# First image of phase 1: a hand-written order, a norm on VectorE and ScalarE, and v's bias outside the matmuls

## The chip, the core and the metric

The kernel runs on one core of one Trainium2 chip. The metric is the device time of one execution in microseconds (us), and the comparison is made on the median of several runs. The engines are called by the profile's names: PE is TensorE (PEld its weight loads), DVE is VectorE, ACT is ScalarE, POOL is GpSimd, SP is SyncE, which here only issues DMAs. Each engine executes its own queue in order.

## What is computed

Two attention layers follow each other on x of shape (8, 512, 32, 32). The change touches only the first step of the first layer: group norm, the q, k and v projections, and the extremes of q, k and v, which the quantisation afterwards needs. Cut to that:

```python
h = group_norm(x.reshape(b, c, T), gn_w, gn_b)          # 32 groups of 16 channels, T = 1024
qkv = jnp.einsum('oc,bct->bot', qkv_w, h) + qkv_b[None, :, None]
q, k, v = jnp.split(qkv.reshape(b * NUM_HEADS, -1, T), 3, axis=1)
q, k, v = fake_quant(q), fake_quant(k), fake_quant(v)   # 8 bits, scale from the whole tensor's min and max
w = softmax(einsum('bct,bcs->bts', q * scale, k * scale))
```

The scale of each quantisation comes from all of q, k or v, so q, k and v of all eight images are computed and stored to DRAM first (phase 1), and attention starts only then.

## The kernel before

**Tiles.** The channels of an image are 4 chunks of 128 partitions (`CC = 4`), its 1024 tokens two halves (`hf`, 512 each). The loop over images and halves is at the end of phase 1 (from line 675); within a half it calls `blocks` (line 663). A block is one output tile of 128x512. For q and k a block is a group of 128 output channels, for v it is 128 tokens. A matmul of the projection is done with split operands: `split_weights` (line 424) and `split_half` (line 435) make of weights and normed x a high part (ACT), a low part and a mix (DVE, two rows each), and for the weights ACT scales the low part. `three` (line 487) then does 8 matmuls into a bank `a` and 4 into a bank `m`; `put` (line 499) has ACT make u from bank a, with the scale -(SH+1) and a bias, and DVE combine u with bank m and take the running maximum. `store` (line 507) takes the minimum on DVE and issues the store on SP. PSUM is one pool of eight banks (`one`, line 393).

**Image 0.** Two of the four q groups and two of the four k groups are done with unsplit matmuls in fp32 (`qk_mm`, line 587: four fp32 matmuls over the chunks per tile, each of which the trace shows as two), since these don't need the split weights. The rest of image 0 is done as blocks (`blocks`, line 663, where b is 0): in each half two q, two k and four v blocks. The later images have twelve blocks in each half. The first two tiles of q (`early`) run chunk by chunk, while the norm of the next chunk is still under way: `norm_steps` (line 225) takes the statistics of a chunk (`bn_stats`, twice, and an aggregate, on DVE), averages over the groups with a matmul against `gavg` (gps), forms the deviation with four small DVE rows, averages again (gps2), adds eps (DVE), takes the power -0.5 on POOL (line 260), multiplies by the weight and applies mean and scale to x on DVE, two halves of 512.

**Biases.** `bias(i)` (line 564) folds the norm's bias into q's, k's and v's: four matmuls of 32 columns (wt), a copy by ACT, and a sum over channels (wc, q and k) or rows (wr, v). For v the result is written in fp32r as `vrow`: high part in partitions 0 to 31, the remainder in 32 to 63. `pick` is a matrix with two rows of ones. `v_block` (line 527) passes `(pick, vrow)` to `three` as a ninth matmul of bank a:

```python
pairs.insert(0, first)          # line 492: the bias as a matmul of its own, in v blocks alone
```

**Order.** PE's order is the program's: `mm` chains each matmul to the last (line 206). The other engines' orders are made when the kernel is built, by a scheduler that takes rows whose inputs it holds for ready. `InOrder` (line 72) wraps DVE, ACT and PE; only if `InOrder.planned` is set does it chain each instruction to the one before. In phase 1 before the change it isn't set. What order there is comes from generators: `several` (line 611) yields the steps of the split of half 0, six weight parts and half 1, and `go` takes steps of it between blocks; `norm(b + 1)` (as `ahead`) is taken a step per block, so that the two averages of image 1 stand in PE's queue between blocks of image 0. `dve.after(normed)` keeps the splits of image 0 behind its norm. SP takes its DMAs in order. At the start these are x and weights of q by chunks (lines 420, 422), the weights of k and v (line 545), then x of image 1; v's bias is loaded from ACT's queue. Two buffers of the pool `raw` hold the bias stage first, and later the first q and k of phase 2, which SP loads ahead.

## Time and profile before

| | us |
|---|---|
| median of 3 runs (lowest, highest) | 2612.9 (2612.3, 2613.9) |
| the profiled execution, its own time | 2613.4 |
| its span in the trace | 2611.6 |
| phase 1, from the start to the last v block of image 7 | about 591 |
| PE busy of the span | 2546.6 (98%) |
| DVE, ACT, POOL busy | 1863.7 (71%), 1389.8 (53%), 195.3 (7%) |

In the trace all instructions of DVE and ACT carry line 91 (the recording wrapper) and all matmuls line 206, so instructions are told apart by the tiles they write and read: `qkps<-x,raw_w` is an unsplit matmul of image 0, `qkps<-half,w_high` a split one, `vps<-vrow,pick` the bias of v, `gps_a` an average over groups, `gst_a` a statistics row, `gmv_a` an aggregate, `u_ring` and `u_last` the tile u. A matmul's length in the trace overlaps that of the next, so distances are taken from start to start. The granted clock of PE is given as a share of full speed. "Idle before" is the time in which the engine had nothing before this row, and the name behind it what ended that.

### The profile page before, as it was taken

To read this page: it belongs to the slowest core of one execution; us is meant where nothing else is said; L and a number is where in the kernel's file an instruction comes from. 1 tells how busy PE (TensorE), PEld (TensorE's weight loads), DVE (VectorE), ACT (ScalarE), POOL (GpSimd) and SP (SyncE) were. 2 spreads that over 40 slices of the span, in tenths; PEclk is the share of its full clock that TensorE was granted. 3 is DMA by queue.
4 is the path that set the end of the run, shared out by engine and by line. 5 is a ranking of instruction groups with operands and counts; after the bars stand their busy time and mean duration, and the time that the engine had idled before them with its cause. 6 is when DMAs were issued, how large, how long until landed. Compare 5 with 4: busy or idle time off the path is not lost.

```text
span 2611.6 us, 38765 instructions
## 1 busy us (share of the span) xinstructions
PE 2546.6 (98%) x15670; PEld 1763.3 (68%) x15670; DVE 1863.7 (71%) x2675; ACT 1389.8 (53%) x1750; POOL 195.3 (7%) x160
## 2 busy tenths in 40 slices
PE   7899999998989999999999999999999999999998
PEld 4788888882236775776677577757766775777687
DVE  7766666558777777877777777778777776776544
ACT  3333333326866674666576566746665765664121
POOL 0000000001110001000100010010001000100000
PEclk9999999999999999999999999999999999999999
DMA  5333233333421222223312322322232123212211
GB/s 177 142 123 112 112 117 129 122 125 102 137 67 44 64 98 92 76 86 102 102 46 78 122 82 66 106 82 86 74 109 98 54 78 118 86 46 89 86 37 38
DMA packets 154958, 242.05 MB, mean 93 GB/s; under 512 B 26512, under 2 KB 92048, under 8 KB 153232
## 3 DMA queue, kind: packets, MB, share of 16 engines
q1 hardware_dynamic: 124064, 181.50, 21.2%
q10 hardware_dynamic: 30704, 57.97, 6.5%
q8 instruction: 125, 2.05, 0.3%
q14 instruction: 65, 0.53, 0.1%
HBM read 152.59 MB, written 86.28 MB: 91 GB/s over the span
## 4 chain that ended last, share of the span: by engine, by line
PE 88%; DVE 4%; ACT 3%; issue 2%; DMA 1%; POOL 0%; SPq 0%; ACTq 0%; DVEq 0%; POOLq 0%
PE s L206 15%; PE o L206 13%; PE qkps L206 13%; PE pj L206 9%; PE av L206 8%; PE v2ps L206 7%; PE vps L206 7%; PE g L206 7%; PE st L206 4%; PE sm L206 4%; ACT pt L91 1%; PE fold L206 1%; DVE two L91 1%; DVE acc L91 1%; ACT aside L91 1%
## 5 line engine op out<-in xcount | busy, mean ns | idle before, releaser
L91 ACT ACTIVATE pt<-st,esc 128x1024 f32<-128x1024 f32 x496 | 526.8, 1114 | 344.1 <-PE st L206 325.0
L91 DVE TENSOR_TENSOR two<-pt,two 128x1024 f16<-128x1024 f32 x496 | 596.9, 1220 | 134.1 <-POOL two L906 110.0
L91 ACT CAST two<-pt 128x1024 f16<-128x1024 f32 x358 | 362.3, 1056 | 5.1 <-ACT p L91 5.1
L906 POOL CAST two<-pt 128x1024 f16<-128x1024 f32 x128 | 169.8, 1327 | 1545.4 <-ACT pt L91 780.6
L206 PE MATMUL av<-two,v 128*32 128x512 f16 x3968 | 244.7, 381 | 0.0
L206 PE MATMUL s<-g,h 128*128 128x256 f32 x1024 | 233.4, 380 | 0.0
L206 PE MATMUL pj<-ao,wp 128*128 128x512 f32 x512 | 223.8, 595 | 0.0
L206 PEld LDWEIGHTS s<-g,h 128*128 128x128 f32 x1024 | 192.9, 190 | 31.0 <-issue 4.3
L206 PE MATMUL st<-q,k 64*128 64x512 bf16 x1024 | 164.0, 383 | 25.0 <-ACT pt L91 12.9
L206 PEld LDWEIGHTS <-v 128*32 128x32 f16 x3968 | 91.2, 96 | 136.3 <-issue 63.4
L206 PE MATMUL s<-g,sums 128*128 128x256 f32 x768 | 178.5, 381 | 0.2 <-DVE p L91 0.2
L206 PEld LDWEIGHTS pj<-ao,wp 128*128 128x128 f32 x512 | 96.0, 190 | 121.5 <-issue 111.3
L206 PE MATMUL o<-p,v 128*128 128x256 f32 x768 | 175.2, 382 | 0.9 <-DVE p L91 0.9
L206 PEld LDWEIGHTS o<-p,v 128*128 128x128 f32 x768 | 144.3, 190 | 27.1 <-issue 5.7
L206 PEld LDWEIGHTS s<-g,sums 128*128 128x128 f32 x768 | 144.5, 190 | 24.4 <-issue 4.6
L206 PE MATMUL sm<-two,ones 128*32 128x512 f16 x1984 | 136.2, 379 | 0.6 <-ACT rs L91 0.6
L91 ACT ACTIVATE u_ring<-qkps,qkbt 128x512 f32<-128x512 f32 x89 | 60.9, 684 | 140.4 <-PE qkps L206 130.7
L206 PEld LDWEIGHTS <-k 64*128 64x128 bf16 x1024 | 34.7, 94 | 147.8 <-issue 144.6
L206 PE MATMUL qkps<-half,w_high 128*128 128x512 f32 x480 | 130.5, 394 | 0.0
L206 PE MATMUL qkps<-half,w_mix 128*128 128x512 f32 x480 | 129.5, 392 | 0.0
L206 PE MATMUL qkps<-half,w_low 128*128 128x512 f32 x480 | 129.4, 391 | 0.0
L206 PE MATMUL g<-h,wa 128*128 128x256 f32 x512 | 122.7, 388 | 2.0 <-DVE h L91 1.9
(209 smaller groups left out, 3871.3 us busy)
## 6 DMA issues: line engine op xcount, KB each, us to landing
rs<-rs_d SPq DMA_DIRECT2D x80, 256.0 KB
x<-in_x_dram SPq DMA_DIRECT2D x32, 512.0 KB
q_d<-wa SPq DMA_DIRECT2D x32, 512.0 KB
k_d<-wa SPq DMA_DIRECT2D x32, 512.0 KB
raw<-q_d SPq DMA_DIRECT2D x32, 512.0 KB
raw<-k_d SPq DMA_DIRECT2D x32, 512.0 KB
v_d<-v_ring SPq DMA_DIRECT2D x32, 512.0 KB
x_d<-h SPq DMA_DIRECT2D x64, 256.0 KB
```

The costliest lines, as they stand in the source:

```text
L91: ins = self.latest = op(*args, **kw).ins
L206: ins = nc.tensor.matmul(ps, lhsT=lhsT, rhs=rhs, **kw).ins
L906: copy(two[:, 0], pt)
```

## The change

1. `InOrder.planned` is set from before the first load to the end of image 0's first half, so DVE and ACT keep the written order among the rows of that stretch; rows of what comes afterwards are still placed by the scheduler. The order itself is written out: per chunk `stats0`, `centre0`, `spread0`, then splits, weight parts, extractions and stores.
2. In image 0's norm the power on POOL is replaced: ACT takes the square root, DVE the reciprocal and one correcting step (`spread0`); mean and scale are applied by ACT, but for chunk 0's first half. The later images keep POOL's power.
3. The first halves of q's and k's weights (512 KB each) are not split in image 0. `load_rest` loads them again, into the two buffers of the pool `raw`, and `split_rest` splits them as a side job of image 1's first half. So that image 1 doesn't need them at once, images from 1 on take the group pairs in the order 1, 0.
4. v's bias: no matmul with `pick`; `vrow` holds -SH times the bias in fp32 in all partitions, and `put` has DVE make u for v, with `vrow` as a full operand. For q and k u stays with ACT.
5. The load of v's bias goes from ACT's queue to SP's, behind the weights; three memsets on POOL and two copies on ACT are gone.

The weight sums `wt`, `wc` of k and `wt`, `wr` of v are called in other places of PE's order. The diff, cut to what the text speaks of:

```diff
-            def three(nm, left, right, first=None):
+            def three(nm, left, right):
 
                 a, m = (one(f"{nm}_{i}") for i in range(2))
                 pairs = [(left[i][cc], right[i][cc]) for i in range(2) for cc in range(CC)]
-                if first is not None:
-                    pairs.insert(0, first)
                 for i, (lt, rt) in enumerate(pairs):
                     mm(a, lhsT=lt, rhs=rt, start=(i == 0), stop=(i == len(pairs) - 1))
                 for cc in range(CC):
...
             def put(dst, a, m, bias, name):
                 i = turn_of("u", 3)
                 u = u_ring[:, i, :] if i < 2 else u_last
-                act.activation(u, a, AF.Identity, bias=bias, scale=-(SH + 1.0))
+                if name == "vmax":
+                    dve.scalar_tensor_tensor(u, a, -(SH + 1.0), bias, ALU.mult, ALU.add)
+                else:
+                    act.activation(u, a, AF.Identity, bias=bias, scale=-(SH + 1.0))
...
-                        (pick, vrow),
                     )
-                    put(t[:, i, :], a, x, 0.0, "vmax")
+                    put(t[:, i, :], a, x, vrow, "vmax")
                     yield
...
+            InOrder.planned = True
             load_x(0)
...
-            act.dma_start(vb, vbias[0:1, :].partition_broadcast(P))
+            nc.sync.dma_start(vb, vbias[0:1, :].partition_broadcast(P))
...
                 if i == 2:
                     dve.tensor_add(vb, vb, by_row())
-                    dve.tensor_scalar(vb, vb, SH / (SH + 1.0), None, ALU.mult)
-                    act.copy(vrow, vb)
-                    dve.tensor_tensor(
-                        vrow[32:64, :], vb[32:64, :], vrow[32:64, :].bitcast(F32), ALU.subtract
-                    )
+                    dve.tensor_scalar(vrow, vb, -SH, None, ALU.mult)
                     return
...
+            def centre0(c):
+                d, mean, *_ = cols0(c)
+                ps = one(f"gps_a0_{c}")[:, 0:1]
+                mm(ps, lhsT=gavg, rhs=mv0[:, c, 0:1], start=True, stop=True)
+                dve.tensor_sub(d, mv0[:, c, 0:1], ps)
+                dve.tensor_copy(mean, ps)
+                dve.tensor_mul(d, d, d)
+                dve.tensor_add(d, d, mv0[:, c, 1:2])
+
+            def spread0(c):
+                d, mean, var, root, rstd, step, off = cols0(c)
+                ps = one(f"gps2_a0_{c}")[:, 0:1]
+                mm(ps, lhsT=gavg, rhs=d, start=True, stop=True)
+                act.activation(root, ps, AF.Sqrt, bias=eps)
+                dve.tensor_scalar(var, ps, EPS, None, ALU.add)
+                dve.reciprocal(rstd, root)
+                dve.scalar_tensor_tensor(step, var, rstd, rstd, ALU.mult, ALU.mult)
+                dve.tensor_scalar(step, step, -0.5, 1.5, ALU.mult, ALU.add)
+                dve.scalar_tensor_tensor(
+                    rstd, rstd, vec[:, V_GN0W + c : V_GN0W + c + 1], step, ALU.mult, ALU.mult
+                )
+                dve.scalar_tensor_tensor(off, mean, -1.0, rstd, ALU.mult, ALU.mult)
+                for hf in range(NH):
+                    xx = x0[:, c, bass.ts(hf, 512)]
+                    if (c, hf) == (0, 0):
+                        dve.tensor_scalar(xx, xx, rstd, off, ALU.mult, ALU.add)
+                    else:
+                        act.activation(xx, xx, AF.Identity, bias=off, scale=rstd)
...
-            part = norm(0, CC)
-            early = [[one(f"qkps_0_{t}_{hf}") for hf in range(NH)] for t in range(2)]
-            for g in (*part, part[0], part[0], part[1]):
-                next(g)
-            bq, bk, bv = (bias(i) for i in range(3))
-            then = iter((part[1], part[2], part[2], part[3], part[3]))
-            for cc in range(CC):
-                for t in range(2):
-                    for hf in range(NH):
-                        qk_mm(early[t], t, hf, cc)
-                        if (cc, hf) in ((0, 1), (1, 0), (1, 1)):
-                            next(next(then, iter(())), None)
-                            normed = dve.latest
-                if cc >= 2:
-                    next(bq, None)
...
+            first = split_half(0, 0)
+            stats0(0, 0)
+            stats0(0, 1)
+            centre0(0)
+            stats0(1, 0)
+            spread0(0)
+            stats0(1, 1)
+            centre0(1)
+            stats0(2, 0)
+            early_mm(0, 0)
+            spread0(1)
+            early_mm(0, 1)
+            stats0(2, 1)
+            centre0(2)
+            stats0(3, 0)
+            first[0]()
+            early_mm(1, 0)
+            spread0(2)
+            early_mm(1, 1)
+            stats0(3, 1)
+            centre0(3)
+            first[1]()
+            early_mm(2, 0)
+            spread0(3)
+            next(bq)
+            early_mm(2, 1)
+            first[3]()
+            first[2]()
+            parts[0][0]()
+            parts[1][0]()
+            first[4]()
+            early_mm(3, 0)
+            early_mm(3, 1)
+            first[5]()
+            next(bq, None)
+            parts[0][1]()
+            parts[2][0]()
+            parts[3][0]()
+            parts[1][1]()
+            outs = [[out_tile() for _ in range(NH)]]
+            late = [one(f"qkps_0_{PAIRS}_{hf}") for hf in range(NH)]
+            for hf in range(NH):
+                for cc in range(CC):
+                    qk_mm(late, PAIRS, hf, cc)
+            for t in range(2):
+                for hf in range(NH):
+                    out_of(early[t], outs[0], t, hf)
+            next(bk)
+            parts[0][2]()
+            parts[1][2]()
+            parts[2][1]()
+            next(bk, None)
+            keep(outs[0], 0, 0)
+            outs.append([out_tile() for _ in range(NH)])
+            last = [one(f"qkps_0_{PAIRS + 1}_{hf}") for hf in range(NH)]
+            for hf in range(NH):
+                for cc in range(CC):
+                    qk_mm(last, PAIRS + 1, hf, cc)
+            for hf in range(NH):
+                out_of(late, outs[1], PAIRS, hf)
+            next(bv)
+            parts[2][2]()
+            parts[3][1]()
+            parts[3][2]()
+            next(bv, None)
+            second = split_half(0, 1)
+            for step in second[:3]:
+                step()
+            keep(outs[0], 0, 1)
+            for hf in range(NH):
+                out_of(last, outs[1], PAIRS + 1, hf)
+
+            def chores():
+                keep(outs[1], 1, 0)
+                yield
+                yield from one_by_one(second[3:])
+                keep(outs[1], 1, 1)
+                yield
+
...
+            rest = []
+
+            def load_rest():
+                for i in range(2):
+                    t = raw_p.tile([P, T], F32, tag="raw", name=f"rest_{i}").rearrange(
+                        "p (c n) -> p c n", c=CC
+                    )
+                    cs = slice(i * C, i * C + C // 2)
+                    nc.sync.dma_start(t, w_qkv[:, :, cs])
+                    rest.append(split_weights(t, slice(0, CC), cs))
+
+            def split_rest():
+                for i in range(2):
+                    rest[i][0]()
                     yield
-                yield from split_half(0, 1)
-
-            more = several()
+                    rest[i][1]()
+                    yield
+                    rest[i][2]()
...
-            go(more, 6)
-            for isk in range(2):
-                outs = [out_tile() for _ in range(NH)]
-                for t in range(2):
-                    if isk:
-                        ps = [one(f"qkps_0_{PAIRS + t}_{hf}") for hf in range(NH)]
-                        for hf in range(NH):
-                            for cc in range(CC):
-                                qk_mm(ps, PAIRS + t, hf, cc)
-                    else:
-                        ps = early[t]
-                    if (isk, t) == (0, 1):
-                        go(bk)
-                    elif (isk, t) == (1, 0):
-                        go(bk)
-                        go(bv)
-                    elif (isk, t) == (1, 1):
-                        go(bv)
-                    c = isk * PAIRS + t
-                    for hf in range(NH):
-                        dve.tensor_scalar(
-                            outs[hf][:, t, :], ps[hf], qkb[:, c : c + 1], None,
-                            ALU.add, ALU.max, accum_out=column("kmax" if isk else "qmax"),
-                        )
...
             def blocks(b, hf):
                 if b == 0:
@@ -667,7 +777,7 @@
                     for n in range(2):
                         yield from v_block(b, hf, n)
                     return
-                for m in range(2):
+                for m in (1, 0):
...
-                            side = [more, more, ahead]
+                            ahead = behind(3, ahead)
+                            side = [chores(), ahead]
                         else:
-                            side = [split_half(b, 1), ahead]
+                            side = [one_by_one(split_half(b, 1)), ahead]
+                            if b == 1:
+                                side.insert(0, split_rest())
...
+                        if b == 0:
+                            load_rest()
...
+                InOrder.planned = False
```

## The prediction

> **What bounds the kernel now.** I read the share of each engine by stretches first. Columns: stretch, its length, then busy time and instruction count of PE, PEld, DVE, ACT and POOL, the granted PE clock, the DMA share, GB/s.
>
> ```profile
> 15.00:53.00 38.00, 36.82 (x115) 16.56 (x116) 31.12 (x63) 13.47 (x15) 1.65 (x3) 1.00 0.35 132
> 53.00:67.60 14.60, 14.60 (x63) 11.45 (x61) 14.44 (x24) 7.76 (x10) 0.00 (x0) 1.00 0.44 144
> 67.60:74.50 6.90, 0.06 (x1) 0.01 (x1) 6.90 (x13) 0.00 (x0) 0.00 (x0) 0.72 0.55 166
> 110.00:590.00 480.00, 479.94 (x2095) 390.99 (x2094) 305.85 (x585) 161.01 (x217) 6.05 (x6) 1.00 0.33 123
> ```
>
> From 110 to 590 us (images 1 to 7 of phase 1) PE never rests, and DVE is busy 64%: here time is what PE has to do. In image 0 it is otherwise: DVE is full from 53 to 74.5, and PE stands for 6.9 us. The list of waits and the timeline say for whom (columns: start, length, engine, what, idle before it and its releaser):
>
> ```profile
> PE gps_a L206 <- DVE gmv_a L91: 16.0, 3, 7.0
> ```
>
> ```profile
> 13.46 0.54 POOL L260 TENSOR_TENSOR grstd_a<-grstd_a,mhalf 128x1 f32<-128x1 f32 x1
> ...
> 14.83 3.78 PE L206 MATMUL qkps<-x,raw_w 128*128 128x512 f32 x4 [3.29 <-DVE x L91]
> ...
> 53.07 1.49 PE L206 MATMUL qkps<-half,w_high 128*128 128x512 f32 x4
> ...
> 53.67 0.69 DVE L91 TENSOR_TENSOR stage<-stage,wr 128x512 f32<-128x512 f32 x1
> ...
> 74.18 0.20 DVE L91 BATCH_NORM_AGGREGATE gmv_a<-gst_a 128x2 f32<-128x12 f32 x1
> ...
> 74.52 0.56 PE L206 MATMUL gps_a<-gmv_a,gavg 128*128 128x4 f32 x2 [6.86 <-DVE gmv_a L91]
> ...
> 75.51 1.91 PE L206 MATMUL vps<-w_high,half 128*128 128x512 f32 x4
> ```
>
> PE executes in order. The group average of image 1 (gps_a) stands in its queue in the middle of image 0, and its input is the last of a long DVE list. After the stop the four matmuls take 1.91 us, later 1.09.
>
> The steady part, one v block to the next:
>
> ```profile
> 207.64 0.39 PE L206 MATMUL vps<-vrow,pick 128*128 128x512 f32 x1
> 207.87 1.10 PE L206 MATMUL vps<-w_high,half 128*128 128x512 f32 x4
> ...
> 209.74 1.09 PE L206 MATMUL vps<-w_mix,half 128*128 128x512 f32 x4
> ...
> 210.67 0.40 PE L206 MATMUL vps<-vrow,pick 128*128 128x512 f32 x1
> ```
>
> A v block takes 3.03 us, and the bias matmul 0.23 of it (207.64 to 207.87; lengths overlap, so starts are compared).
>
> **What the Trainium skill says.** "TensorE: Matmul & The Clock Gate", section "What's actually happening": after an idle window of about 3.4 us the array runs at half clock until it has been busy as long again. The trace agrees: half speed from 14.83 to 18.6, and from 75.1 to 80.8. "VectorE: DVE Perf Modes", "Why PSUM operands drop a tier": an fp32 operand in PSUM holds DVE at one element a cycle. The trace agrees: PSUM plus SBUF at 128x512 is 0.69 us (53.67 above), a plain SBUF multiplication of that size 0.42. "ScalarE: Activation LUTs", "What ACT_TABLE_LOAD costs" and "Table sets: the hidden batching unit": 1.28 us and a drain of 1.38 for each change of set, and exp and sqrt are in different sets. The trace has one load of 1.28 us; no run shows the drain.
>
> **The change, part by part.** Times are those of the profiled execution, 2613.4 us (span 2611.6), 0.5 above the median 2612.9; differences carry over to the median. Orders are those of the built program.
>
> *v's bias.* 64 matmuls go, 8 in image 0. In images 1 to 7: 56 x 0.23 = 12.9 us off a PE that never rests. In return u of the v blocks moves from ACT (0.60 us) to DVE. The trace has no such instruction; the nearest row is 0.69 us (start to start 0.61, the next row begins at 54.28). Bounds 0.6 and 0.8; I take 0.65. That is 56 x 0.65 = 36 us, and DVE goes from 306 of 480 to some 340 of 467, 73%. Its cover is the eight PSUM banks, four blocks of two: PE may run on while a u is late. Cost taken: 0. Without this cover each us of lateness would be one of PE.
>
> *Norm of chunk 0 without GpSimd.* Before, the power waits for GpSimd, whose first result starts at 12.73, and PE begins at 14.83. After: the second average is there at 8.8 as before, ACT takes the root (0.3, between 0.2 and 0.5). DVE first has a statistics row of chunk 1, whose data came at 9.37; v's bias no longer loads ahead of it (256 KB), so about 8.9. Then 0.65 + six small rows 0.9 + half of x 0.55 = 11.05. But PE's queue has the first average of chunk 1 ahead, which needs one more statistics row and the aggregate (0.8): 11.9, and 0.6 for it. **PE begins at 12.5**, 2.3 us sooner.
>
> *The rounds after it.* A round is: average (0.3), four small rows (0.65), meanwhile two half-tile matmuls, second average (0.25), root (0.3), six small rows (0.9), statistics and aggregate (0.8). The root stands behind the two matmuls in PE's order, so DVE idles here; in return ACT, not DVE, applies seven of eight halves (DVE saves 7 x 0.54). Aggregates come at 11.9, 18.6 (half clock) and 22.9, chunk 2's second pair ends at 27.8, chunk 3's four at 31.2. Before: 34.9. Gain 3.7.
>
> *Weight sums for k and v* now stand directly ahead of what reads them: wt, copy on ACT (0.6 with its wait), wc. PE waits 0.65 us twice. Before, 7 us of matmuls lay between. PE from 31.2: wc 0.85, eight matmuls 6.9, wt 0.95, 0.65, wc 0.85, 6.9, wt 0.95, 0.65, wr 0.86 = 19.6. So **the split blocks begin at 50.8**, before 53.07.
>
> *What DVE has left then.* The row that adds wr to v's bias now stands ahead of all of hf 1's split, so DVE waits for wr about 3 us, until 50.8. From there to the last aggregate of image 1, by DVE's order, start-to-start times of the trace: 12 rows of 1024 (two split pairs, w_low and w_mix of the moved q weights, which the scheduler pulls in here, six minima) x 1.135 = 13.6; two extractions 1.3; seven maxima 4.4; three u 1.95; statistics 14 x 0.60 = 8.4 (six of image 2, pulled in too); six aggregates 0.7; bias rows 0.9; a wait for ACT's `half`, behind two w_low scalings, 1.2. Sum **32.5 us: 83.3**. Before: 53.67 to 74.3, 20.6 us.
>
> *What that makes late.* gps_a now stands after all eight blocks. PE has them done at 50.8 + 4 x 2.75 + 4 x 2.8 = 73, and then stands about **10 us**, to 83.3. The average takes 0.6, hf 1 begins at 83.9, at half clock for 5.7 us as before: 2.85 lost, so it counts as 86.75. Before, hf 1 began at 87.01 at full clock. **The first half of image 0 gains 0.25 us**: the start's gain goes into the longer stop. Then image 1's norm is late: applied by ACT from 92.1 (before 83.8), its last split row at 113.0, by the same addition; image 1's first block starts at 109.0 and wants it at 111.7, and a low part 0.35 sooner. **Loss 1.65 us**, taken whole.
>
> *Queues.* SP gets two 512 KB weight loads ahead of k's first stores; the load that prefetches phase 2's first q waits for their split, and image 2's x stands behind that. DVE reads image 2 six rows after its buffer is free, 6 us; in the trace such a load was read 4.6 us after issue without a wait. Cost 0; if it were 3 us late, 3 us. The root on ACT is followed by nothing urgent. The power of the later images stays on GpSimd.
>
> *End of phase 1.* A second table load stands ahead of the first exp. ACT is idle from 600.1 to 601.5 there, so 1.28 us fits; with the skill's drain, 1.3 late. On the other side the last v maximum has one row of 0.69 less ahead of it: 0.5. Taken: 0, bounds -0.5 and 1.3.
>
> Sum: 12.9 + 0.25 - 1.65 = 11.5; 2613.4 - 11.5 = 2601.9, against the median **2601.4**.
>
> **Rivals.** *A: the start keeps its gain.* Were DVE's list no longer than before beyond PE's blocks (a stop of 7 us, no wait in image 1), it would be 12.9 + 8 x 0.23 + 2.3 = 17: 2596. For it: my rows may be long by 5%, 1.6 us. Against it: the counted rows. *B: image 0 loses more.* Loads of image 2 or the moved weights land late, or chunk 1 lands at 9.4: 3 to 6 us, 2606. For it: DVE waits in order, and all of its list is critical. *C: slower than before.* DVE's u in the v blocks: bank a comes free only when DVE gets to it. It decides from the point where DVE is more than two blocks (5.6 us) behind PE; were each of the 56 delayed by 0.5 us, 28 us: 2629. Against it: DVE in the steady part shows idle times of 1 to 2 us in most blocks, so it catches up. *D: no change*, if image 0 loses all the 11.5: 2613. That the matmuls are gone is plain from the program.
>
> **Numbers.** Forecast 60%, own range 2597.5 to 2604; A 19%, B 13%, C 4%, D 4%. Likeliest 2601.4. The range goes down to A's 2595 and up past B to 2607.5. Measurement tells about 0.2%, 5 us: faster by more is below 2607.7, that is forecast, A and most of B: 0.90; within 0.06; slower 0.04.
>
> **What would show it.** A v block of 2.80 us, PE full from 115 to the end of phase 1; PE's first x matmul near 12.5 and split blocks near 50.8; one stop of PE of about 10 us ahead of gps_a, half clock after it; a pause near 110; a table load at the end of the phase with pt right behind. Wrong it would be by a v block of over 2.9 us with PE waiting for DVE's u, or by a stop that is not there.

## The result, and the profile after

| | before | changed |
|---|---|---|
| median of 8 runs each | 2613.4 us (2610.7 to 2616.2) | 2605.9 us (2604.1 to 2606.6) |
| ratio, 95% interval | | 0.9969 (0.9958 to 0.998) |
| span of the profiled execution | 2611.6 us | 2604.0 us |

The change makes the kernel 0.3% faster: 7.5 us by the medians, 7.6 between the two profiled executions. The prediction was 2601.4 us, 11.5 us less than before, in a range of 2595 to 2607.5; its forecast proper, without the rivals, reached from 2597.5 to 2604.

First the share of each engine by stretches of the changed kernel (stretch, length, busy time and count of PE, PEld, DVE, ACT and POOL, granted PE clock, DMA share, GB/s):

```profile
15.00:51.00 36.00, 33.48 (x112) 14.76 (x112) 26.15 (x60) 14.94 (x21) 0.00 (x0) 1.00 0.30 116
51.00:73.00 22.00, 22.00 (x95) 17.52 (x94) 20.57 (x33) 9.05 (x11) 0.00 (x0) 1.00 0.80 264
73.00:83.50 10.50, 1.01 (x5) 0.48 (x3) 10.50 (x25) 0.00 (x0) 0.00 (x0) 0.68 0.18 71
110.00:580.00 470.00, 467.98 (x2027) 379.31 (x2028) 339.42 (x637) 126.28 (x161) 6.04 (x6) 1.00 0.34 125
```

DVE has gone from 64% to 72% of the steady part and PE is still full there, as predicted. The stop of PE in image 0 is now 73 to 83.5, while DVE works through. PE's list of waits in the first 600 us (what waits, for what, sum, times, longest), and its timeline in image 0:

```profile
PE gps_a L206 <- DVE gmv_a L91: 20.3, 5, 9.5
...
PE qkps L206 <- DVE half L91: 1.6, 2, 1.1
...
PE gps_a L206 <- DVE gd_a L91: 1.0, 2, 0.5
PE wr L206 <- ACT stage L91: 0.8, 1, 0.8
PE wc L206 <- ACT stage L91: 0.7, 1, 0.7
```

```profile
12.01 2.91 PE L206 MATMUL qkps<-x,raw_w 128*128 128x512 f32 x3
...
51.24 1.50 PE L206 MATMUL qkps<-half,w_high 128*128 128x512 f32 x4
...
83.54 0.59 PE L206 MATMUL gps_a<-gmv_a,gavg 128*128 128x4 f32 x2 [9.53 <-DVE gmv_a L91]
83.98 2.05 PE L206 MATMUL qkps<-half,w_high 128*128 128x512 f32 x4
85.84 1.64 PE L206 MATMUL qkps<-half,w_low 128*128 128x512 f32 x4
...
107.91 1.10 PE L206 MATMUL qkps<-half,w_high 128*128 128x512 f32 x4
...
110.00 0.74 PE L206 MATMUL qkps<-half,w_low 128*128 128x512 f32 x2 [0.53 <-DVE half L91]
...
112.27 0.74 PE L206 MATMUL qkps<-half,w_mix 128*128 128x512 f32 x2 [1.05 <-DVE half L91]
112.84 0.85 PE L206 MATMUL qkps<-half,w_high 128*128 128x512 f32 x3
```

The start is there at 12.01 and the split blocks at 51.24; the gain is gone at 83.54, after a stop of 9.53 us; four matmuls take 1.86 us from there to 85.84, about half speed; 110.00 and 112.27 are image 1 waiting for its split rows. At 112.84 image 1's second block begins. In the kernel before, the first block of image 1 began at 110.12 and took 2.75, so its second began at 112.87. **At this point the two kernels are level.** The line of before, and then DVE's side in the changed kernel:

```profile
110.12 1.09 PE L206 MATMUL qkps<-half,w_high 128*128 128x512 f32 x4
```


```profile
51.84 0.69 DVE L91 TENSOR_TENSOR stage<-stage,wr 128x512 f32<-128x512 f32 x1 [4.09 <-PE wr L206]
...
83.30 0.19 DVE L91 BATCH_NORM_AGGREGATE gmv_a<-gst_a 128x2 f32<-128x12 f32 x1
```

**Where the 7.6 us come from.** The marks below are starts in the profiled executions. "Folding" is the first matmul after the last v block of phase 1.

| | image 0's second half | image 1's first block | its first v group | folding | folding to the end |
|---|---|---|---|---|---|
| before | 87.01 | 110.12 | 121.12 | 592.37 | 2019.2 |
| changed | 83.98 | 107.91 | 121.09 | 583.14 | 2020.8 |

Image 0 gives nothing, images 1 to 7 give 9.2 us, and 1.6 us are lost after phase 1. From image 1 on PE takes turns: a q/k group of four blocks (48 matmuls), then a v group of two blocks (24 matmuls). The 9.2 need a closer look, because the v groups do shrink as predicted: from 6.05 to 5.60 us each, and 28 of them make 12.6 us. What takes back 3.4? The timeline of PE in the changed kernel, a q/k group at 144.51 and the next at 161.31:

```profile
141.71 1.09 PE L206 MATMUL vps<-w_high,half 128*128 128x512 f32 x4
142.65 1.09 PE L206 MATMUL vps<-w_low,half 128*128 128x512 f32 x4
143.58 1.10 PE L206 MATMUL vps<-w_mix,half 128*128 128x512 f32 x4
144.51 1.10 PE L206 MATMUL qkps<-half,w_high 128*128 128x512 f32 x4
145.45 1.10 PE L206 MATMUL qkps<-half,w_low 128*128 128x512 f32 x4
146.38 1.10 PE L206 MATMUL qkps<-half,w_mix 128*128 128x512 f32 x4
...
161.31 1.09 PE L206 MATMUL qkps<-half,w_high 128*128 128x512 f32 x4
162.24 1.08 PE L206 MATMUL qkps<-half,w_low 128*128 128x512 f32 x4
163.16 1.07 PE L206 MATMUL qkps<-half,w_mix 128*128 128x512 f32 x4
```

Read the starts, not the lengths. From 145.45 to 146.38 four matmuls take 0.93 us, 233 ns each; from 162.24 to 163.16 they take 0.92, and over the whole group 229. The same group in the kernel before (it starts at 145.02), 0.92 us for four:

```profile
145.95 1.08 PE L206 MATMUL qkps<-half,w_low 128*128 128x512 f32 x4
146.87 1.07 PE L206 MATMUL qkps<-half,w_mix 128*128 128x512 f32 x4
```

There all q/k groups of 48 matmuls take 11.00 us, or 11.09 behind an average of the next image's norm; in the changed kernel 13 of them take 11.20 (144.51 is the first, 548.25 the last), with the granted clock at 1.00 and no wait in the list. That is 2.6 us. Two v groups with a part of the next image's norm in them also stop for DVE's `gd_a` (1.0 us for the two in the list of waits), so that 0.45 + 0.70 us of the 12.6 do not arrive. Ahead of the first stop, at 127.6 us, DVE has waited 1.35 us for a load of x; ahead of the second, at 464.5, a row of u stands before the last row of `gd_a`. 12.6 - 2.6 - 1.15 = 8.85; the rest to 9.2 is rounding and the step to the folding.

### The profile page after: what moved, and what is told of

Same layout as the page of the kernel before. It is cut to its first block, busy times and chain, and to the rows that moved or that the text cites. A ratio compares the mean times of both kernels' runs of the same rounds, so it can differ in the third digit from the quotient of the medians.

```text
span 2604.0 us, 38580 instructions
## 1 busy us (share of the span) xinstructions
PE 2532.2 (97%) x15606; PEld 1750.0 (67%) x15606; DVE 1905.0 (73%) x2748; ACT 1358.1 (52%) x1696; POOL 194.1 (7%) x153
## 4 chain that ended last, share of the span: by engine, by line
PE 85%; DVE 4%; ACT 3%; issue 2%; DMA 2%; POOL 0%; SPq 0%; ACTq 0%; DVEq 0%
PE s L206 15%; PE o L206 14%; PE qkps L206 11%; PE pj L206 9%; PE av L206 8%; PE v2ps L206 7%; PE g L206 7%; PE vps L206 5%; PE st L206 4%; PE sm L206 4%; ACT pt L91 1%; PE fold L206 1%; DVE two L91 1%; ACT aside L91 0%; DVE acc L91 0%
```

## The experiments

All ratios are to the kernel before, run on the same chip as the variant: its median was 2612.6 us beside experiments 1 to 4, 2613.1 beside 5 to 8 and 2612.5 beside 9 to 12. The theory I started from: PE's matmuls have two paces, and the pace is handed on from group to group; the bias matmul used to break the chain. The rivals: the pace belongs to the new order of the column halves (`for m in (1, 0)`), or to the place in the half image.

**1. v's bias by VectorE, alone** (on the kernel before).

```
-                act.activation(u, a, AF.Identity, bias=bias, scale=-(SH + 1.0))
+                if name == "vmax":
+                    dve.scalar_tensor_tensor(u, a, -(SH + 1.0), bias, ALU.mult, ALU.add)
+                else:
+                    act.activation(u, a, AF.Identity, bias=bias, scale=-(SH + 1.0))
...
-                        (pick, vrow),
-                    put(t[:, i, :], a, x, 0.0, "vmax")
+                    put(t[:, i, :], a, x, vrow, "vmax")
...
+                    dve.tensor_scalar(vrow, vb, -SH, None, ALU.mult)
```

> The kernel before, with v's bias added by VectorE and nothing else of the change. Theory (the pace of the q and k matmuls is handed over from block to block: a v group of 24 equal matmuls leaves every second q/k group at 233 ns a matmul, and the bias matmul, which stood ahead of each v block, used to bring it back to 229): 12.6 us come off images 1 to 7, about 2.6 of them are lost again to q/k groups at 233 ns, and image 0 loses some 1.5 because its list on VectorE gets 2 us longer: about 2605, with half of the q/k groups of images 2 to 7 at 11.20 us instead of 11.00. Rival (the slower pace belongs to the new order of the two halves of the q and k columns, and not to the bias): all q/k groups stay at 11.00 us, and the time is about 2602.5.

Measured: 2601.7 us, ratio 0.9965 (0.9952 to 0.9979). 13 q/k groups take 11.20 us, with the column halves in their old order: the rival falls. But image 0 did not lose 1.5 us, it gained 2.7: image 1's first v group starts here:

```profile
118.42 1.10 PE L206 MATMUL vps<-w_high,half 128*128 128x512 f32 x4
```

Before, it was 121.12. 1.9 us of that come from image 0's first v group and 0.9 from its second. My fear that u on DVE would lengthen the stop was wrong: it is 6.3 us here, before 6.9.

**2. The order of image 0 without the bias** (on the changed kernel; the bias matmul, its `pick` and its `vrow` as before).

```
+                        (pick, vrow),
-                    put(t[:, i, :], a, x, vrow, "vmax")
+                    put(t[:, i, :], a, x, 0.0, "vmax")
...
+            act.copy(pick, picked)
```

> The changed kernel with v's bias back as a matmul on TensorE: only the new order of image 0, the split of weights in image 1, and the swapped order of column halves are left. Theory: all q/k groups are at 11.00 us again, v groups at 6.05; image 0 gains about 1 us, because its list on VectorE is 2 us shorter than in the changed kernel; about 2612, no difference that counts. Rival (the pace belongs to the order of the column halves): every second q/k group stays at 11.20 us and the time is about 2615.

Measured: 2620.0 us, ratio 1.0028 (1.0017 to 1.004). All q/k groups but those of image 0 and image 1's first are at 11.00 to 11.09, as the theory has it, but this run does not isolate the order: my edit put a wait at the head of it. ACT and DVE at the start:

```profile
14.66 0.43 POOL L568 MEMSET stage<- 1x128 f32 x2
15.12 0.30 ACT L91 CAST pick<-stage 128x128 fp32r<-128x128 f32 x1 [12.67 <-POOL stage L568]
15.44 1.28 ACT L91 ACT_TABLE_LOAD   x1
16.73 0.26 ACT L91 ACTIVATE root<-gps_a,eps 128x1 f32<-128x1 f32 x1
17.03 0.16 DVE L91 TENSOR_SCALAR var<-gps_a 128x1 f32<-128x1 f32 x1 [8.39 <-ACT root L91]
```

In a written order ACT cannot take the root before the copy ahead of it, the copy waits for GpSimd, and DVE loses 8.4 us. The split blocks began at 59.48 instead of 51.24.

**3. The column halves in the old order** (on the changed kernel).

```
-                for m in (1, 0):
+                for m in (1, 0) if (b, hf) == (1, 0) else (0, 1):
```

> The changed kernel, with the column halves of the q and k weights in the order of before (first, second) from the second half of image 1 on. Theory (handed-over pace): the slow q/k groups stay where they were, the first group of each half image, whichever columns it reads; time as the changed kernel, 2605.9. Rival (the second half of the columns, by its place in memory, is read more slowly): the slow groups move to the second place of each half image.

Measured: 2605.0 us, ratio 0.9973 (0.9962 to 0.9985). Neither text is right in full. In image 1 the slow group was the second of the half image, from 211.99 on it was the first, and after a v group with a stop for `gd_a` (458.33, 6.67 us instead of 5.97) there was no slow group any more up to the end of the phase, though nothing interrupted PE any further. So the pace is bound neither to the columns nor to the place: a pattern that is there goes on, which is what "handed on" means. Behind an interruption it can change but need not: in the changed kernel the v group at 458.10 has the same stop and the same 6.67 us, and every second group stays slow after it.

**4. VectorE's later rows held back** (on the changed kernel; `first_norm[0]` is the row that writes image 1's `goff`).

```
                     dve.bn_stats(st[:, i, hf, :], src(cc, hf))
+                    if nm == "a2":
+                        dve.after(first_norm[0])
...
                     dve.tensor_tensor(low, raw, high.bitcast(F32), ALU.subtract)
+                    if wait:
+                        dve.after(first_norm[0])
```

> The changed kernel; VectorE's statistics rows of image 2 and its rows that split the remaining q and k weights are held back until image 1's norm has its factors. Theory (TensorE's stop in image 0 is set by VectorE's list alone): some 6 us of rows leave that list, image 1's last aggregate comes at about 77.2 instead of 83.3, the second half of image 0 starts at about 78, image 1's first block 3 to 6 us sooner; about 2601. Rival (the rows that were held back meet the splits of image 1 in turn, so that image 1 starts no sooner): the stop is shorter, but image 1's second block still starts at about 112.8, and the time is 2605.9.

Measured: 2606.7 us, ratio 0.9981 (0.9972 to 0.9989). The rival is right. Image 0's second half starts at 79.59 (changed: 83.98), image 1's first block at 104.28 (107.91), and then PE stands for image 1's second pair of split rows:

```profile
104.28 1.10 PE L206 MATMUL qkps<-half,w_high 128*128 128x512 f32 x4
105.22 0.62 PE L206 MATMUL qkps<-half,w_low 128*128 128x512 f32 x2
110.13 1.22 PE L206 MATMUL qkps<-half,w_low 128*128 128x512 f32 x2 [4.29 <-DVE half L91]
```

Its first v group starts at 122.42, 1.3 us later than in the changed kernel. The rows that left one stretch met the next one.

**5. DVE does not wait for wr** (on the changed kernel).

```
             next(bv)
-            parts[2][2]()
             parts[3][1]()
+            second = split_half(0, 1)
+            second[0]()
+            parts[2][2]()
             parts[3][2]()
-            next(bv, None)
-            second = split_half(0, 1)
-            for step in second[:3]:
-                step()
             keep(outs[0], 0, 1)
             for hf in range(NH):
                 out_of(last, outs[1], PAIRS + 1, hf)
+            second[1]()
+            second[2]()
+            next(bv, None)
```

> The changed kernel, in which VectorE takes the rows that wait for wr (v's bias) behind the minimum, the maxima and the first split pair of image 0's second half, and ScalarE writes that half's first part ahead of two scalings of w_low. Theory (what image 0 loses is VectorE's idle time ahead of wr, 4.1 us, plus 0.5 for the split's input): its list to image 1's last aggregate ends some 3.4 us sooner, at about 80; image 1's second block starts at about 109.4 instead of 112.84; about 2602.5. Rival (as in the run with rows held back: what sets image 1's start is the whole of VectorE's rows up to there, and idle time of VectorE later on grows by the same amount): image 1's second block stays at 112.8 and the time at 2606.

Measured: 2607.6 us, ratio 0.9975 (0.9967 to 0.9984); image 1's first v group starts at 124.80. The wait for wr is gone, and DVE's list is no shorter: one row waits 1.83 us for a load of x, one 0.56 us for PE, one 1.39 us for ACT's `half` (0.52 in the changed kernel), and ahead of image 1's last aggregate stand an aggregate of image 2 and a row of the remaining weights, 1.2 us. DVE at its end:

```profile
82.73 0.19 DVE L91 BATCH_NORM_AGGREGATE gmv_a<-gst_a 128x2 f32<-128x12 f32 x1
82.84 1.17 DVE L91 TENSOR_TENSOR w_low<-rest,w_high 128x1024 fp32r<-128x1024 f32 x1
83.93 0.20 DVE L91 BATCH_NORM_AGGREGATE gmv_a<-gst_a 128x2 f32<-128x12 f32 x1
```

Part of what is freed goes to other waits, part to a row that the scheduler puts in. My theory gave no place to either, and fell.

**6. A small matmul in the v group** (on the changed kernel).

```
                 a, m = (one(f"{nm}_{i}") for i in range(2))
+                if kick:
+                    mm(a[:, 0:4], lhsT=gavg, rhs=vec[:, 0:4], start=True, stop=True)
...
+                        kick=b > 0 and (n, i) == (0, 1),
```

> The changed kernel with one more matmul of four columns (a group average of constants, written to a bank that the block then overwrites; it leaves nothing out) ahead of the last v block of each half image from image 1 on. Theory (handed-over pace: a matmul of another shape inside the v group ends the lock, as the bias matmul did): all q/k groups of images 1 to 7 at 11.00 us, 13 x 0.2 = 2.6 us gained against 14 x 0.09 = 1.3 us for the added matmuls: about 2604.5, and the trace decides. Rival (the pace depends on the mean length of a v group, or on something else than a matmul of another shape): the slow groups at 11.20 us stay, and the time is about 2607.

Measured: 2606.3 us, ratio 0.9972 (0.9962 to 0.9983). **From image 1's second q/k group on each of them takes 11.00 us** (11.09 in those behind a norm's average). PE's timeline across the added matmul into the group that was slow:

```profile
141.86 0.28 PE L206 MATMUL vps<-vec,gavg 128*128 128x4 f32 x2
142.00 1.18 PE L206 MATMUL vps<-w_high,half 128*128 128x512 f32 x4
...
144.88 1.09 PE L206 MATMUL qkps<-half,w_high 128*128 128x512 f32 x4
145.80 1.08 PE L206 MATMUL qkps<-half,w_low 128*128 128x512 f32 x4
146.72 1.08 PE L206 MATMUL qkps<-half,w_mix 128*128 128x512 f32 x4
```

Its price was mis-estimated: the v group grows from 5.60 to 5.82, by 0.22 us and not 0.09, so that 14 of them take 3.1 us for 2.6.

**7. The same on the first experiment**: v's bias by VectorE in the old order, with `kick=b > 0 and (n, i) == (1, 1)`.

> The kernel before with v's bias added by VectorE (the first experiment) and the matmul of four columns ahead of the last v block of each half image from image 1 on. Theory: the q/k groups are all at 11.00 us, some 1.3 us net faster than the first experiment: about 2600.5. Rival: slow groups stay; about 2603.

Measured: 2603.9 us, ratio 0.9962 (0.9949 to 0.9976). One slow group is left, image 1's first, ahead of the first added matmul. The folding begins at 579.89, against 579.68 without the matmul: here too its price (3.1 us by the figure above) is more than its gain of 2.6.

**8. The order of image 0 alone, mended**: as 2, with the copy moved.

```
-            act.copy(pick, picked)
...
+                    act.copy(pick, picked)
                     act.copy(vrow, vb)
```

> As the second experiment (the changed kernel with v's bias as a matmul again), but with ScalarE's copy of the selecting matrix moved from the start to just ahead of v's bias, so that ScalarE's root no longer stands behind it. Theory: PE's first matmul on x is at about 12 us again, all q/k groups at 11.00 us; the order of image 0 alone is worth about nothing: image 1's second block starts at 111 to 113, and the time is about 2612. Rival (the written order is worth its 2.3 us of earlier start): about 2610.

Measured: 2613.9 us, ratio 1.0004 (0.9996 to 1.0012). The theory is right: no difference. Image 1's first v group starts at 120.41, 0.7 us sooner than before. All q/k groups of images 2 to 7 are at 11.00 or 11.09 but one, at 402.69, which follows a v group with a stop (7.49 us): even with the bias matmul an interruption can hand on the slow pace.

**9. Experiments 4 and 5 together.**

> The changed kernel with both edits: rows of image 2 and of the remaining weights held back until image 1's norm (fourth experiment), and v's bias rows behind the maxima and the first split pair (fifth). Theory (VectorE is full from 52 us to image 1's second block, and only work taken out of that stretch, here 3.4 us of idle time, moves its end): image 0's second half starts at about 76 and image 1's first v group at about 119.0, where it was 122.42 with the rows held back alone and 121.09 in the changed kernel; about 2602.5. Rival (image 1 is then late for another reason, ScalarE or a DMA): v group at 121 or later, time 2605 or more.

Measured: 2606.2 us, ratio 0.9972 (0.996 to 0.9983); second half at 78.67, image 1's first block at 103.44, its first v group at 121.60. The rival is right again, and what PE waits for is the same as in 4:

```profile
109.30 1.22 PE L206 MATMUL qkps<-half,w_low 128*128 128x512 f32 x2 [4.30 <-DVE half L91]
```

So 3.4 us less idle time on DVE at 50 us do not start image 1 sooner. Its split rows come one to each v step, with other rows between them; I did not try another order of these.

**10. A smaller matmul** (on the first experiment).

```
+                    mm(a[:, 0:4], lhsT=wsp[0][:, 0, 0:P], rhs=wsp[0][:, 0, 0:4], start=True, stop=True)
```

> The kernel before with v's bias by VectorE, and ahead of the last v block of each half image from image 1 on a matmul of four columns in fp32r instead of fp32 (it leaves nothing out). Theory (any matmul of another shape ends the lock, and this one costs some 0.06 us instead of 0.22): all q/k groups at 11.00 us, the start of phase 1's last part 1.5 us sooner than in the first experiment (579.68), about 2600. Rival (the lock ends only by the time that the added matmul takes): the slow groups stay, time 2602.5.

Measured: 2603.7 us, ratio 0.9961 (0.9948 to 0.9975). Between the two texts: it costs 0.1 us, and 9 slow groups are left (image 1's first, ahead of the first added matmul, and eight behind it) where there were 13, now in other places. A matmul of another shape does not end the slow pace every time; the four-column fp32 one did.

**11. Another order of equal matmuls** (on the first experiment; in the last v block of a half image w_mix goes first).

```
+                if not turned:
+                    sums()
                 for cc in range(CC):
                     mm(m, lhsT=left[2][cc], rhs=right[2][cc], start=(cc == 0), stop=(cc == CC - 1))
+                if turned:
+                    sums()
```

> The kernel before with v's bias by VectorE; in the last v block of each half image from image 1 on the four matmuls with w_mix go ahead of the eight with w_high and w_low. No matmul is added. Theory (it takes a matmul of another shape): the slow groups stay at 11.20 us, about 2602. Rival (a change in which operand follows which is enough): all q/k groups at 11.00 us, 2.6 us off, about 2599.5.

Measured: 2602.6 us, ratio 0.9957 (0.9944 to 0.9971). The theory is right: the slow groups stay, from 140.22 to 543.25.

**12. The changed kernel again.**

> The changed kernel once more, unaltered, to see how far its phase 2 varies from one execution to another. Theory (the 1.7 us that it lost after phase 1 against the kernel before are chance, a DMA that landed late and a stretch at half clock): phase 1's last part starts at 583 us again, and what follows it is within 2018 to 2022 us, not the same 2020.8. Rival (VectorE's new order at the end of phase 1 costs it each time): the round trip through memory in image 0 of phase 2 is late by 0.8 us again and PE waits 1.2 us for it again.

Measured: 2605.9 us, ratio 0.9969 (0.9957 to 0.9981). The unchanged program gave the cleanest evidence on the pace. Up to 447 us its q/k groups are slow where they were; then PE stops 0.44 us for `gd_a` in the v group at 458.06, and from there on all are fast. The first execution has the same stop, 0.44 us at the same place, and goes on as before it. The same instruction in the two executions, first the one shown at the top, then this one:

```profile
481.45 1.10 PE L206 MATMUL qkps<-half,w_high 128*128 128x512 f32 x4
482.38 1.10 PE L206 MATMUL qkps<-half,w_low 128*128 128x512 f32 x4
483.32 1.10 PE L206 MATMUL qkps<-half,w_mix 128*128 128x512 f32 x4
```

```profile
481.41 1.09 PE L206 MATMUL qkps<-half,w_high 128*128 128x512 f32 x4
482.33 1.08 PE L206 MATMUL qkps<-half,w_low 128*128 128x512 f32 x4
483.25 1.08 PE L206 MATMUL qkps<-half,w_mix 128*128 128x512 f32 x4
```

One program, one place, two paces: columns, addresses or order alone cannot decide it. The two executions differ in timing, and perhaps in the chip, so that PE's relation in time to another engine remains a rival that no run excludes.

The single starts in the traces show the state one group earlier. In the eleven executions without the bias matmul, the last matmuls of a v group ahead of a slow q/k group start evenly, some 233 ns apart give or take 1 (105 of 106 cases, counted from image 1's second group on); ahead of all 191 fast ones their distances alternate around 231 and 236 ns. Without a norm's average or an added matmul the v group takes 5.60 us either way. So the state that a q/k group takes over can be seen before it begins.

On phase 2: from the folding to the end it took 2022.7 us, not 2020.8 and outside the 2018 to 2022 of the theory; and PE waits for the round trip through memory again, 1.6 us, which was the rival's sign.

The marks side by side (slow groups counted in images 1 to 7; image 1's first has listed waits in the new order and is left out there):

| kernel | second half of image 0 | image 1's first v group | folding | folding to the end | slow q/k groups |
|---|---|---|---|---|---|
| before | 87.01 | 121.12 | 592.37 | 2019.2 | 0 |
| 2 new order, copy at its head | 89.72 | 129.07 | 600.75 | 2018.0 | 0 |
| 8 new order alone | 82.12 | 120.41 | 592.93 | 2020.3 | 1 |
| 1 bias alone | 85.22 | 118.42 | 579.68 | 2019.0 | 13 |
| 11 bias, turned | 83.96 | 117.16 | 578.99 | 2022.5 | 13 |
| 7 bias, small matmul | 84.18 | 117.58 | 579.89 | 2025.9 | 1 |
| 10 bias, smaller matmul | 84.32 | 117.72 | 579.71 | 2022.2 | 9 |
| changed | 83.98 | 121.09 | 583.14 | 2020.8 | 13 |
| changed, again | 84.38 | 121.85 | 582.50 | 2022.7 | 10 |
| 6 changed, small matmul | 84.19 | 122.02 | 583.77 | 2021.5 | 0 |
| 3 changed, old halves | 84.33 | 121.76 | 582.77 | 2019.7 | 10 |
| 4 held back | 79.59 | 122.42 | 583.68 | 2019.1 | 13 |
| 5 wr later | 84.64 | 124.80 | 586.53 | 2021.9 | 13 |
| 9 held back, wr later | 78.67 | 121.60 | 582.87 | 2022.0 | 13 |

**The version that beats both kernels is the smallest part of the change**: v's bias on VectorE with the old order of image 0, 2601.7 us, and 2602.6 in the variant of experiment 11. Against the changed kernel this is 3 to 4 us by the medians. On one chip, experiment 11 took 2601.3 to 2603.5 us in five runs and the changed kernel (experiment 12) 2603.1 to 2607.0 in six. The intervals of the ratios overlap, so that the medians alone don't settle it; the traces do for phase 1: the folding starts at 579.0 to 579.9 in the four with the old order and the bias on VectorE, at 582.5 to 586.5 in the seven executions with the new order and the bias there.

## Why the prediction was right, and where it was not

It was right in the sign, and the time fell inside the range, 4.5 us above the forecast. It lies outside the forecast's own 2597.5 to 2604, in the part of the range that rival B had added, and errors of both signs are in it: of the 12.9 us for v's bias 3.7 did not arrive, image 0 and the start of image 1 came out 1.4 better than forecast, and 1.6 were lost after phase 1 (11.5 - 3.7 + 1.4 - 1.6 = 7.6). By its own steps:

- **v's bias, 12.9 us: the step that failed in size.** The removed matmuls did give what was counted: a v block takes 2.80 us, 28 groups 12.6 us. "PE never rests" was taken to mean that each removed matmul is its own time and leaves the others alone. It does not: what is removed also set the pace of what follows. 2.6 us went to slow q/k groups and 1.15 to two stops for `gd_a`; 9.2 us arrived. The trace of before showed both paces (v matmuls at 233 ns, q/k at 229), and nothing in it said that the faster one depended on the matmul to be removed. That u on DVE would be covered by the eight banks was right: there is no wait of a v block for u. DVE's new load showed elsewhere, in one of the two stops for the norm's small rows.
- **Norm without GpSimd, 12.5: right**, 12.01; the load of x was there a little sooner. Aggregates at 11.3, 17.8 and 22.5 for 11.9, 18.6 and 22.9.
- **Weight sums, split blocks at 50.8: right**, 51.24; the two waits are 0.7 and 0.8 us, not 0.65.
- **DVE's list ends at 83.3: right**, 83.30, though in parts by luck: the wait for wr ended a us later, at 51.84 and not 50.8, the one for ACT's `half` took 0.5 and not 1.2 us.
- **The stop, its half clock, and +0.25 us for the first half: the mechanism was right, the size not.** The stop was 9.53 us for "about 10". Half clock was taken at 5.7 us "as before", 2.85 us lost. The q/k group after the stop took 12.73 us instead of 11.00, so 1.73 us were lost, and the first half gained 1.3 us. In the other kernels with the new order that group took 12.88 to 14.11, after stops of 4.2 to 10.2 us. "TensorE: Matmul & The Clock Gate", section "What's actually happening", says why one length cannot be carried over: the window of about 3.4 us that decides runs freely, so that the moment of the switch shifts from run to run. The measurements here agree: after the restart PE stayed at half clock for 3.5 us in the changed kernel, 6.3 in the kernel before and 6.5 in experiment 5, and the half-clock stretches around this stop are 6.83, 10.24 or 13.65 us long, two, three or four times 3.41.
- **Image 1's norm late, -1.65 us: nearly right in size** (the group took 13.18 instead of 11.00, of which 1.6 us are listed waits and the rest the slower matmuls around them), but the sum left out that image 0's second v group loses its four bias matmuls too, 0.9 us. These 0.9 and the shorter half clock are why image 0 ended level and not 1.4 us behind.
- **Queues at 0**: no wait of PE for one of these loads is listed in the changed kernel. But DVE waits 1.35 us for a load of x just ahead of the first stop for `gd_a` (it waited for x there in the kernel before too, 0.56 us), and 1.83 us in experiment 5, so the cover is thin.
- **End of phase 1 at 0: right at the place itself.** The second table load is there, and `pt`, the first exponential of phase 2, follows 0.2 us after it:

```profile
590.88 1.28 ACT L91 ACT_TABLE_LOAD   x1
...
592.36 2.12 ACT L91 ACTIVATE pt<-st,esc 128x1024 f32<-128x1024 f32 x2 [0.20 <-PE st L206]
```

  It began 0.02 us after the row before it on ACT ended (590.28 + 0.58), and pt starts 0.20 us after its end, as soon as PE delivers, so the drain of 1.38 us, which "ScalarE: Activation LUTs", section "What ACT_TABLE_LOAD costs", had made the bound, shows neither ahead of it nor behind it. Experiment 2 shows the same without PE in between: its load starts 0.02 us after the copy and the root 0.01 us after the load, with DVE waiting for it.
- **Phase 2, not in the sum, took 1.6 us more.** Part of it can be seen: in image 0 of phase 2 PE waits 1.8 us instead of 0.6 for a row behind a round trip through memory. This wait is not scattered: it is 1.1 to 1.8 us in the eight executions that have neither a bias matmul nor an added one in phase 1's v groups, with the old order (experiments 1 and 11) as with the new, and 0.5 to 0.6 in the six that have one. Why is open. The whole time does not follow it: experiment 1 waits 1.4 us and takes 2019.0, experiment 7 waits 0.5 and takes 2025.9. The two executions of the changed kernel are 1.9 us apart, and 14 executions of 13 programs with the same phase 2 spread from 2018.0 to 2025.9. So it is not shown that the change costs the 1.6 us.

Rival A (the start keeps its gain) did not come true: of the start's gain nothing is left at image 1's first v group. Rival B gave 2606, almost the measured time, by image 0 losing 3 to 6 us more; image 0 lost less than forecast, so the number was right for a wrong reason. C and D did not happen.

What image 0 costs was also asked too narrowly. Against the kernel before it is level, but moving its eight biases from PE to DVE is worth 2.7 us in the old order (experiment 1) and nothing in the new: 120.41 without the move, 121.09 and 121.85 with it (experiment 8 and the two executions of the changed kernel). In the new order PE stands for DVE's rows on both sides of this stretch, 9.5 us ahead of the average and 1.6 in image 1, so that matmuls taken from PE in between only lengthen its waits. That is argued and not shown: the eight rows of u on DVE (0.60 us each) come with the move, and no run separates the two. Nor is DVE full there: between 84 and 113 us it waits 3.7 us for ACT's u and 0.5 for GpSimd. What experiments 4, 5 and 9 show is that moving rows or idle time within the stretch moves the place where PE stands and brings image 1's first v group no sooner. What order would do better was not found.

## What to carry to other kernels

When PE is the bound and full, a removed matmul can be worth less than its start-to-start time, by what it did for its neighbours; compare the pace of all groups before and after, not only of the group that was edited. An early start is worth what the next bound engine leaves of it: add up that engine's rows to the first point where both meet, and expect freed time to be taken by other waits, and by rows that a scheduler puts there. Test the smallest part of a change alone, since it may be all of the gain.

## What the runs showed of the hardware

- The 128x128 by 128x512 fp32r matmuls of a q/k group have two steady paces at full granted clock, 229.2 and 233.3 ns (11.00 and 11.20 us for 48). "TensorE: Matmul & The Clock Gate", "Wait — 56ns, not 53.3ns?", gives one for 512 columns back to back, 215.7 ns; these traces show neither that nor a single one. Two patterns go on by themselves: every second group slow (the changed kernel up to 548 us), or all fast (the same program in experiment 12 from 464.73 us on). The same stop of 0.44 us was followed by a change of pattern in one of these executions and not in the other. With a four-column fp32 matmul in each half image all groups behind the first were fast; a four-column fp32r one did that only in part, another order of equal matmuls not at all. What holds this state is open.
- A four-column fp32 matmul between full ones lengthens its v group by 0.22 us (5.60 to 5.82), a four-column fp32r one by 0.1 (to 5.70).
- After the stop in image 0, 4.2 to 10.2 us long, PE stayed at half clock for another 3.5 to 6.5 us in the 14 executions, and the longer time does not go with the longer stop (3.5 after 9.53 us, 6.3 after 6.86).
- DVE's multiply-and-add with one operand in PSUM and one in SBUF at 128x512 lasts 0.63 to 0.69 us; the next row begins 0.60 us after its start when it waits for nothing. The prediction took 0.65. Its comparison, 0.69 us with PSUM against 0.42 for a multiplication in SBUF, sets two operands against one: additions of two fp32 operands that both lie in SBUF take 0.69 us at this size too (`acc<-acc,p`, later in the kernel). So these traces do not show that PSUM is what costs.
